# First loads of the outlook on GpSimd, rows measured beside the experts, and two queues in written order

## The chip, the cores and the metric

The kernel runs on one core of a Trainium2 chip. Its time is the device time of that core, in microseconds (us); a comparison takes the median of several runs. TensorE (PE) multiplies and transposes, VectorE (DVE) and ScalarE (ACT) work on whole tiles, GpSimd (POOL) and SyncE (SP) here mostly issue DMAs.

## The reference

Two layers of a vision network on x of 4 x 32 x 32 x 384, in float32. Layer 0 is an attention with a chosen set of keys, then four experts of which each token takes two. Layer 1, where the change lies, is an "outlook" attention and a small feed-forward network whose weights are Kronecker products:

```python
x = x + _L0_conv_ref(_ln_c(x), qkv_w, gp_w, proj_w)      # attention
t = t + _L0_ffn_ref(_ln_t(t), gate_w, gate_b, w1, b1, w2, b2)   # experts: each token takes 2 of 4
x = x + _L1_conv_ref(_ln_c(x), Wv, Wa, Wo)               # outlook
t = t + _L1_ffn_ref(_ln_t(t), c_fc_1, c_fc_2, c_proj_1, c_proj_2)   # Kronecker

# outlook
v = x @ Wv.T ; a = (x @ Wa.T).reshape(b, n, heads, 9, 9)
attn = softmax(a * d ** -0.5)
out[p] = sum over q of attn[p, q] * v[q]   # 3 x 3 patches; q, p are places of a patch
y = sum over p of out[p] shifted by p ; return y @ Wo.T
```

_ln_c is a layer norm over the 384 channels: mean and variance of each row, then (x - mean) / sqrt(variance + eps).

## The kernel before

The 4096 rows of x are 32 tiles of 128 rows, eight tiles to an image. Four stages follow each other: the attention (to about 1290 us), the experts (35 blocks of 256 gathered rows, 31.68 us each, to 2431.6), the outlook (to about 2911) and the Kronecker network (to 3007).

**Experts.** `experts` walks over the blocks. For each it fetches, one block ahead, the weights `up` and `down` with indirect DMAs on GpSimd (`weights`, L1486), the rows (`fetch`, L1507), norms and turns them (`norm` L1516, `turn`), and then multiplies: L1568 with gelu L1572, and L1583, whose result gets its bias at L1588 on VectorE and is stored to `yg` on SyncE (L1589). Weights lie in two sets of buffers, `halves`. Beside the blocks, `add` (L1532) takes a tile of x from `x1`, gathers its two expert rows (`router.gather`, L1452, on GpSimd), adds them with their weights (L1538) and stores the sum to `x2` (L1539). One tile a block is done so, once its image is complete: `done` = 19 tiles. The order of TensorE, VectorE, ScalarE and SyncE in attention and experts is the written one (`manual_schedule`); GpSimd's is set by a planner.

**Between the stages.** `rest` gives places in memory to x of the four images and the weights, then loads them: `fetch(0)`, `wa`, `wv`, `fetch(1)`, `wo`, `fetch(2)`, `fetch(3)`, and the Kronecker weights (`wf` four times, `wp`, `f2` and `p2`), all on SyncE (L95, L2101, L1897 to L1900).

**Outlook.** The planner sets the order on every engine here, from costs and dependencies. The loop at the end of `outlook` walks over 32 steps (image b, tile t), and nine more to drain. In a step:

- `add` (from step 2): one of the 13 tiles that the experts left (tiles 19 to 31) gets its two expert rows, gathered into one of two buffers `yt`, L1665 on VectorE.
- `scores`: norm of the tile (L127), three transposes into `ps_tr` (L135), copy to `xnT` (L136, ScalarE), twelve matmuls to `ps_a` (L1693), of which there is one buffer; maximum and subtraction (L1702, L1703) free it and give `attn`; exponential on ScalarE (L1708), sums, reciprocal and product (L1710 to L1717); `attn` is moved by 32 partitions up and down with three or four DMAs on SyncE (L1729 to L1734); `ps_v` (L1737) and its copy (L1741).
- `band`, two steps later: `u` adds the moved copies (L1750 to L1754), nine small matmuls with the `shift` matrices to `ps_c` (L1758), `co` masks with `inside` (L1766), is written to DRAM (`room`, L1773) and read back skewed (`band`, L1779), both on SyncE.
- `gather`, three steps after that: ps_y (L1795) multiplies band and v; some rows are split, so that narrow matmuls of 66 columns occur.
- `mix`: ps_wo (L1811), and its sum into x (L1815).

The layer norm's statistics are taken for a whole image at a time: `ln_stats` measures eight tiles on VectorE (bn_stats L120, bn_aggr L121), takes the square root on ScalarE (L122) and the reciprocal (L123). For image 0 this is ahead of step 0, for the others in step 4 of the image before:

```python
        stats[0] = net.ln_stats(range(NB), "c")
...
                if t == 4 and b + 1 < B:
                    stats[b + 1] = net.ln_stats(range((b + 1) * NB, (b + 2) * NB), "c")
```

The constants (`shift`, `col`, `inside`) are made on GpSimd and VectorE at the head of `outlook`.

Of the kernel before, what the change touches and what calls it, by code (L numbers as in the profile page):

```python
# [47 lines left out]
class Net:  # L48
# [12 lines left out]

    def slots(self, dram):
# [27 lines left out]
    def load(self, x, tiles=range(NT)):  # L90

        i = tiles.start
        while i < tiles.stop:
            n = min(NB - i % NB, tiles.stop - i)
            self.nc.sync.dma_start(  # L95
# [17 lines left out]
    def stats(self, tiles, key):  # L113

        nc, n = self.nc, len(tiles)
        mv = self.small.tile([P, NT, 2], FP, name="ln_mv", tag="ln_mv")
        rs = self.small.tile([P, NT], FP, name="ln_rs", tag="ln_rs")
# [6 lines left out]
        return mv, rs  # L124

# [1332 lines left out]
def experts(net, router, x1, x2, wup, wdown, beside):  # L1458
# [10 lines left out]
    with ExitStack() as ctx:  # L1469
# [78 lines left out]
        for n in range(NXB):  # L1548
# [27 lines left out]
            if n + 1 < NXB:  # L1576
                norm(n + 1)
            for t in range(TT):
# [17 lines left out]
def outlook(net, wv, wa, wo, left, router, kron):  # L1596
# [15 lines left out]
    with ExitStack() as ctx:  # L1612
# [13 lines left out]
        for dx in (-1, 0, 1):  # L1626
# [34 lines left out]
        def add(i):  # L1661
            for n in range(2):
# [4 lines left out]
                )  # L1667

        stats = {}
# [527 lines left out]
```

## Time and profile before

| what | value |
|---|---|
| runs | 3003.22, 3002.94, 3001.56 us; median 3002.94 |
| profiled execution | 3008.57 us |
| its span | 3006.7 us (1.87 lie around it) |
| mean granted clock of TensorE | 0.971 |
| TensorE busy | 2793.6 us, 93% of the span |
| VectorE, ScalarE, GpSimd busy | 1344.4, 1222.3, 396.4 us |
| outlook | 2431.6 to about 2911 us of the span |

A start time in the profile counts from the begin of the span. A line of the timeline gives start, length, engine, source line, operation, what it writes and reads, sizes and count; in brackets at its end stands how long the engine had been idle before it and what released it. A matmul of 128x486 is a stationary tile of 128 x 128 on 486 columns. `SPq` is SyncE issuing a DMA; a long issue means that the issue itself took that long, not the transfer.

### The profile page before, as it was taken

The page shows a single profiled execution, that of the slowest core. Times are in us where ns is not written, and L with a number is a line of the kernel's source. Part 1 is how long each engine was busy: PE and PEld are TensorE (multiplying, and loading weights), DVE is VectorE, ACT ScalarE, POOL GpSimd, SP SyncE. Part 2 cuts the span into 40 slices and gives each one's busy share as a digit, 9 for nine tenths or more (in the row PEclk, how much of TensorE's full clock was granted, in tenths as well). Part 3 has the DMA queues.
Part 4 walks back from the last instruction along what each step waited for, and adds up shares of the span by engine and source line. Part 5 has one row for each costly group of instructions (what it writes and reads, how often), then busy time and mean ns, then how long its engine had stood idle before and what let it go on. Part 6 is the DMA issues. An engine that isn't in the chain of part 4 may idle for free.

```text
span 3006.7 us, 36661 instructions
## 1 busy us (share of the span) xinstructions
PE 2793.6 (93%) x13236; PEld 1509.9 (50%) x13236; DVE 1344.4 (45%) x3704; ACT 1222.3 (41%) x2026; POOL 396.4 (13%) x496
## 2 busy tenths in 40 slices
PE   6879998999899986689999999999999978999998
PEld 4323333333333331156777777777777744444443
DVE  1466677766776676633010001111111147767652
ACT  3777777776767765321112112111121122222125
POOL 1000000200030004014111112212211012000000
PEclk9989999999999998899999999999999989999999
DMA  5133334322322233254445545555555455544432
GB/s 100 52 81 98 92 92 122 78 54 68 93 56 54 77 90 118 49 200 155 169 177 189 186 174 204 213 211 196 201 215 210 142 170 190 163 165 139 157 112 86
DMA packets 218111, 405.91 MB, mean 135 GB/s; under 512 B 83504, under 2 KB 179296, under 8 KB 204864
## 3 DMA queue, kind: packets, MB, share of 16 engines
q1 hardware_dynamic: 188496, 194.43, 21.7%
q0 software_dynamic: 26432, 206.01, 20.1%
q10 hardware_dynamic: 2992, 3.03, 0.3%
q8 instruction: 107, 1.75, 0.2%
q14 instruction: 84, 0.69, 0.1%
HBM read 305.35 MB, written 49.99 MB: 118 GB/s over the span
## 4 chain that ended last, share of the span: by engine, by line
PE 78%; ACT 7%; DVE 6%; DMA 5%; issue 4%; POOL 0%; SPq 0%; DVEq 0%; POOLq 0%; ACTq 0%
PE ps_h L1568 18%; PE ps_y L1583 17%; PE ps_t L266 7%; PE ps_z L615 7%; PE ps_s L597 6%; PE ps_o L615 5%; PE ps_a L1693 4%; ACT e L607 4%; PE ps_y L1795 3%; DVE e L653 2%; PE ps_wo L1811 2%; DMA yt<-yg,index 2%; PE ps_v L1737 1%; PE ps_h L1964 1%; PE ps_t L400 1%
## 5 line engine op out<-in xcount | busy, mean ns | idle before, releaser
L1572 ACT ACTIVATE h<-ps_h,up 128x256 f32<-128x256 f32 x420 | 199.0, 474 | 929.2 <-PE ps_h L1568 929.2
L1568 PE MATMUL ps_h<-xbT,up 128*128 128x256 f32 x2520 | 556.8, 382 | 0.8 <-DVE xbT L1527 0.7
L1583 PE MATMUL ps_y<-down,h 128*128 128x384 f32 x1680 | 556.8, 489 | 0.0
L1568 PEld LDWEIGHTS ps_h<-xbT,up 128*128 128x128 f32 x2520 | 482.4, 192 | 76.9 <-DVE xbT L1527 1.1
L653 DVE CUSTOM_DVE_ANT_0 e<-e,rz,inv 128x1024 f32<-128x1024 f32 x384 | 474.3, 1272 | 65.1 <-DMA rz<-r_row 64.8
L607 ACT ACTIVATE e<-ps_s,shift 128x1024 f32<-128x1024 f32 x384 | 406.7, 1110 | 192.2 <-PE ps_s L597 191.9
L1583 PEld LDWEIGHTS ps_y<-down,h 128*128 128x128 f32 x1680 | 318.5, 191 | 208.2 <-issue 3.3
L1588 DVE TENSOR_TENSOR y<-ps_y,down 128x384 f32<-128x384 f32 x70 | 39.0, 558 | 755.6 <-PE ps_y L1583 755.6
L615 PE MATMUL ps_z<-e,rt_ones 128*32 128x512 f32 x1536 | 295.1, 631 | 62.8 <-ACT e L607 62.8
L615 PE MATMUL ps_o<-e,wv 128*32 128x512 f32 x1536 | 273.9, 634 | 27.2 <-DVE wv L660 15.6
L597 PE MATMUL ps_s<-q,k 32*128 32x512 f32 x1536 | 222.9, 650 | 0.0
L680 POOL DMA_DIRECT2D q<-po x96 | 75.7, 874 | 1058.2 <-DMA q<-po 622.2
L351 ACT ACTIVATE below<-tk_left,tk_bound 128x1024 bf16<-128x1024 f32 (+1 forms) x160 | 183.8, 1149 | 12.1 <-DVE tk_bound L357 7.6
L1693 PE MATMUL ps_a<-wa,xnT 128*128 128x486 f32 x384 | 172.2, 595 | 10.7 <-DVE attn L1703 10.0
L615 PEld LDWEIGHTS ps_z<-e,rt_ones 128*32 128x32 f32 x1536 | 45.6, 109 | 228.4 <-ACT e L607 190.0
L597 PEld LDWEIGHTS ps_s<-q,k 32*128 32x128 f32 x1536 | 61.5, 187 | 169.5 <-issue 135.1
L615 PEld LDWEIGHTS ps_o<-e,wv 128*32 128x32 f32 x1536 | 66.4, 114 | 150.5 <-issue 108.7
L266 PE MATMUL ps_t<-xnT,wqkv 128*128 128x512 f32 x288 | 138.1, 621 | 2.8 <-ACT tk_left L310 1.8
L1693 PEld LDWEIGHTS ps_a<-wa,xnT 128*128 128x128 f32 x384 | 72.4, 195 | 96.7 <-issue 89.6
L1795 PE MATMUL ps_y<-band,v 128*32 128x194 f32 (+2 forms) x960 | 108.4, 516 | 4.1 <-DMA band<-room 3.9
L1538 DVE SCALAR_TENSOR_TENSOR x<-yt,weight,x 128x384 f32<-128x384 f32 x38 | 23.5, 619 | 191.9 <-DMA x<-x 191.3
L1507 POOL DMA_INDIRECT xb<-x,ids x70 | 66.9, 955 | 251.4 <-PE ps_t L1526 218.4
(331 smaller groups left out, 2860.6 us busy)
## 6 DMA issues: line engine op xcount, KB each, us to landing
band<-room SPq DMA_DIRECT2D x32, 1560.0 KB
rz<-r_row SPq DMA_DIRECT2D x48, 512.0 KB
yg<-y SPq DMA_DIRECT2D x70, 192.0 KB
q<-q SPq DMA_DIRECT2D x192, 64.0 KB
k<-k SPq DMA_DIRECT2D x192, 64.0 KB
room<-none SPq DMA_DIRECT2D x64, 192.0 KB
x<-x SPq DMA_DIRECT2D x38, 192.0 KB
o<-in_x_dram SPq DMA_DIRECT2D x33, 192.0 KB
```

Source lines behind the costliest of these rows:

```text
L266: nc.tensor.matmul(ps, lhsT=lhsT(k), rhs=rhs(k), start=k == 0, stop=k == KC - 1)
L351: nc.scalar.activation(junk[:n], left[:n], AF.Sign, bias=bound[:n], accum_out=over[:n])
L597: nc.tensor.matmul(ps[:, half * 512 : half * 512 + 512], lhsT=self.k4[r, u * P : (u + 1) * P], rhs=self.q4[r, :], start=True, stop=True,)
L607: nc.scalar.activation(e, ps, AF.Exp, bias=shift, scale=QK_SCALE)
L615: nc.tensor.matmul(ps[r : r + 32, :], lhsT=lhsT(odd), rhs=self.es[2 * u + odd][:, half * 512 : half * 512 + 512], start=u == 0, stop=u == ...
L653: nc.vector.tensor_tensor_reduce(self.es[m], self.es[m], self.rz, 1.0, self.im["inv"][:, m, self.h : self.h + 1], ALU.mult, ALU.add, self. ...
L680: nc.gpsimd.dma_start(out=there, in_=po[r : r + 32, :], accum_op=ALU.add)
L1568: nc.tensor.matmul(ps, lhsT=up[:, o : o + P], rhs=xbT[:, k, :], start=k == 0, stop=k == KC - 1,)
L1572: nc.scalar.activation(h, ps, AF.Gelu, bias=up[:, KC * HID + f : KC * HID + f + 1])
L1583: nc.tensor.matmul(ps, lhsT=hs[f][:, t * P : (t + 1) * P], rhs=down[:, f * C : (f + 1) * C], start=f == 0, stop=f == NF - 1,)
L1693: nc.tensor.matmul(pa[:, hh, :HW_], lhsT=xnT[:, k, :], rhs=wa[:, k, hh * HW_ : (hh + 1) * HW_], start=k == 0, stop=k == KC - 1,)
L1795: nc.tensor.matmul(ys[c][32 * n : 32 * n + 32, lo - 512 * half : hi - 512 * half], lhsT=vs[b, t][:, h * HD : (h + 1) * HD], rhs=bands[b, t ...
```

## The change

Four things are done.

1. x of image 0, `wa` and `wv` are loaded on GpSimd's queue. The places in memory are given in another order: Kronecker's small tiles, x of image 0, `wa`, `wv`, `wo`, then the other images.
2. The statistics are taken tile by tile, right after the tile's expert rows are added: for the 19 tiles of the experts in their `add` (`measure`), with one square root and reciprocal in the last block (`scale`); for the other 13 after their `add` in the outlook, with a `scale` whenever an image's tiles are complete. They are kept in `mv` and `rs` for all 32 tiles.
3. In the outlook, SyncE and GpSimd keep the written order (`manual_schedule`); TensorE, VectorE and ScalarE remain with the planner. The remaining loads are written into steps: image 1 and `wo` in step 1, image 2 in step 2, image 3 in step 5, Kronecker's in step 8. So in the written order of SyncE come, in a step, the moves of `attn`, then the step's loads, then `room` and directly `band` of the tile two steps before.
4. The adds of the outlook begin in step 4 instead of step 2, and `col` and `inside` are made after step 0's scores.

Kronecker's own work pool (`kf_work`) is opened in its constructor, and the small buffers of `stats` shrink to its group of 16.

```diff
+        self.mv = cpool.tile([P, NT, 2], FP, name="mv_x2")
+        self.rs = cpool.tile([P, NT], FP, name="rs_x2")
+
...
     def home(self, pool, b):
         self.xs[b] = pool.tile([P, NB, C], FP, name=f"x_{b}", tag=f"x_{b}")
-    def load(self, x, tiles=range(NT)):
+    def load(self, x, tiles=range(NT), queue=None):
         i = tiles.start
         while i < tiles.stop:
             n = min(NB - i % NB, tiles.stop - i)
-            self.nc.sync.dma_start(
+            (queue or self.nc.sync).dma_start(
                 out=self.xs[i // NB][:, i % NB : i % NB + n, :],
                 in_=x[i * P : (i + n) * P, :].rearrange("(t p) c -> p t c", p=P),
             )
...
+
+    def measure(self, pool, i, x):
+
+        st = pool.tile([P, 6], FP, name="x2_st", tag="x2_st")
+        self.nc.vector.bn_stats(st, x)
+        self.nc.vector.bn_aggr(self.mv[:, i, :], st)
+
+    def scale(self, first, last):
+
+        rs = self.rs[:, first:last]
+        self.nc.scalar.activation(rs, self.mv[:, first:last, 1], AF.Sqrt, bias=self.eps["c"])
+        self.nc.vector.reciprocal(rs, rs)
...
                 y = work.tile([P, C], FP, name="yt", tag="yt")
                 router.gather(y, i, n)
                 nc.vector.scalar_tensor_tensor(x, y, router.weight[n][:, i : i + 1], x, ALU.mult, ALU.add)
+            net.measure(work, i, x)
             return lambda: nc.sync.dma_start(out=x2[i * P : (i + 1) * P, :], in_=x)
         added, store = 0, lambda: None
...
                     next(beside, None)
             if n + 1 < NXB:
                 norm(n + 1)
+            else:
+                net.scale(0, added)
             for t in range(TT):
                 if t == TT - 1 and n + 1 < NXB:
                     xbT = turn(n + 1)
...
         inside = const.tile([P, 5 * H6], FP, name="inside")
         col = const.tile([P, 4], FP, name="col")
-        nc.gpsimd.iota(
-            col[:, 0:1], pattern=[[0, 1]], base=0, channel_multiplier=1, allow_small_or_imprecise_dtypes=True,
-        )
-        for r in range(1, P // IMG):
-            nc.vector.tensor_scalar(
-                col[:, r : r + 1], col[:, 0:1], IMG * r - 0.5, -float(IMG), ALU.is_gt, ALU.mult
+        low = const.tile([P, 5 * H6], FP, name="low")
+
+        def columns():
+            nc.gpsimd.iota(
+                col[:, 0:1], pattern=[[0, 1]], base=0, channel_multiplier=1, allow_small_or_imprecise_dtypes=True,
             )
-        for r in range(1, P // IMG):
-            nc.vector.tensor_tensor(col[:, 0:1], col[:, 0:1], col[:, r : r + 1], ALU.add)
-        nc.gpsimd.iota(
-            inside, pattern=[[1, 5], [0, H6]], base=-2, channel_multiplier=0,
-            allow_small_or_imprecise_dtypes=True,
-        )
-        low = const.tile([P, 5 * H6], FP, name="low")
-        nc.vector.tensor_scalar(inside, inside, col[:, 0:1], None, ALU.add)
-        nc.vector.tensor_scalar(low, inside, -0.5, None, ALU.is_gt)
-        nc.vector.tensor_scalar(inside, inside, IMG - 0.5, None, ALU.is_lt)
-        nc.vector.tensor_tensor(inside, inside, low, ALU.mult)
+            for r in range(1, P // IMG):
+                nc.vector.tensor_scalar(
+                    col[:, r : r + 1], col[:, 0:1], IMG * r - 0.5, -float(IMG), ALU.is_gt, ALU.mult
+                )
+            for r in range(1, P // IMG):
+                nc.vector.tensor_tensor(col[:, 0:1], col[:, 0:1], col[:, r : r + 1], ALU.add)
+            nc.gpsimd.iota(
+                inside, pattern=[[1, 5], [0, H6]], base=-2, channel_multiplier=0,
+                allow_small_or_imprecise_dtypes=True,
+            )
+            nc.vector.tensor_scalar(inside, inside, col[:, 0:1], None, ALU.add)
+            nc.vector.tensor_scalar(low, inside, -0.5, None, ALU.is_gt)
+            nc.vector.tensor_scalar(inside, inside, IMG - 0.5, None, ALU.is_lt)
+            nc.vector.tensor_tensor(inside, inside, low, ALU.mult)
         left = list(left)
...
                 nc.vector.scalar_tensor_tensor(
                     net.x(i), y, router.weight[n][:, i : i + 1], net.x(i), ALU.mult, ALU.add
                 )
-
-        stats = {}
+            net.measure(work, i, net.x(i))
+
         attn, vs, bands, ys, moved = {}, {}, {}, {}, {}
         def room(b, t):
...
         def scores(b, t):
             i = b * NB + t
-            mv, rs = stats[b]
             xn = work.tile([P, C], FP, name="xn", tag="xn")
-            net.ln_apply(xn, i, t, mv, rs)
+            net.ln_apply(xn, i, i, net.mv, net.rs)
             xnT = work.tile([P, KC, P], FP, name="xnT", tag="xnT")
             net.transposed(ps_m, "m", xn, xnT, nc.scalar.copy)
             pa = ps_a.tile([P, 2, 512], FP, name="ps_a", tag="a")
...
                 done = b * NB + (4 if half == 0 else 7) + 2 + LAG
                 for n in range(4):
                     at(done + 1 + n // 2, mixed, b, half, n)
-        stats[0] = net.ln_stats(range(NB), "c")
-        t_kron = 0
+        assert left[0] >= 2 * NB
+        t_kron, first = 0, left[0]
         for step in range(B * NB + 9):
             b, t = divmod(step, NB)
-            if step >= 2:
-                for i in left[:1]:
-                    add(i)
-                left = left[1:]
             if b < B:
                 scores(b, t)
-                if t == 4 and b + 1 < B:
-                    stats[b + 1] = net.ln_stats(range((b + 1) * NB, (b + 2) * NB), "c")
+            if step == 0:
+                columns()
+            if step in loads:
+                loads[step]()
+            if step >= 4 and left:
+                add(left.pop(0))
+
+                if left and left[0] % NB == 0 or not left:
+                    net.scale(first, left[0] if left else NT)
+                    first = left[0] if left else NT
             for f, args in later.pop(step, []):
                 f(*args)
             if step == B * NB - 7:
...
         with ExitStack() as late:
-
             pool = late.enter_context(tc.tile_pool(name="late", bufs=1, reuse_waits="tile"))
-            weight = {}
-
-            def home(name, shape):
-                weight[name] = pool.tile(shape, FP, name=name, tag=name)
-
+            kron = Kron(net, late, pool)
             net.xs = {}
-            net.home(pool, B - 1)
-            kron = Kron(net, pool)
             net.home(pool, 0)
-            home("wv", [P, KC, C])
-            kron.home()
-            net.home(pool, 1)
-            net.home(pool, 2)
-            home("wa", [P, KC, 972])
-            home("wo", [P, KC, C])
+            wa, wv, wo = (
+                pool.tile([P, KC, w.shape[-1]], FP, name=n, tag=n)
+                for n, w in (("wa", WaT), ("wv", WvT), ("wo", WoT))
+            )
+            for b in range(1, B):
+                net.home(pool, b)
             def fetch(b):
                 first, last = b * NB, (b + 1) * NB
                 net.load(x2, range(first, min(last, done)))
                 net.load(x1, range(max(first, done), last))
-            def weigh(name, w):
-                nc = tc.nc
-                nc.sync.dma_start(out=weight[name], in_=w.rearrange("(k p) o -> p k o", p=P))
-
-            fetch(0)
-            weigh("wa", WaT)
-            weigh("wv", WvT)
-            for b in range(1, B):
-                fetch(b)
-                if b == 1:
-                    weigh("wo", WoT)
-            kron.load(late, fc1T, fc2, proj1T, proj2)
-            outlook(net, weight["wv"], weight["wa"], weight["wo"], range(done, NT), router, kron)
+            def weigh(queue, tile_, w):
+                queue.dma_start(out=tile_, in_=w.rearrange("(k p) o -> p k o", p=P))
+
+            net.load(x2, range(NB), tc.nc.gpsimd)
+            weigh(tc.nc.gpsimd, wa, WaT)
+            weigh(tc.nc.gpsimd, wv, WvT)
+            loads = {
+                1: lambda: (fetch(1), weigh(tc.nc.sync, wo, WoT)),
+                2: lambda: fetch(2),
+                5: lambda: fetch(3),
+                8: lambda: kron.load(fc1T, fc2, proj1T, proj2),
+            }
+            eng = mybir.EngineType
+            with tc.manual_schedule(engines={eng.SP, eng.Pool}):
+                outlook(net, wv, wa, wo, range(done, NT), router, kron, loads)
             kron.run(out)
     with ExitStack() as outer:
```

More of the change, by code (lines that the diff above doesn't have):

```diff
@@ L115, in stats @@
         nc, n = self.nc, len(tiles)
-        mv = self.small.tile([P, NT, 2], FP, name="ln_mv", tag="ln_mv")
-        rs = self.small.tile([P, NT], FP, name="ln_rs", tag="ln_rs")
+        mv = self.small.tile([P, Kron.GT, 2], FP, name="ln_mv", tag="ln_mv")
+        rs = self.small.tile([P, Kron.GT], FP, name="ln_rs", tag="ln_rs")
         for t, i in enumerate(tiles):
@@ L1593, in experts, with outlook @@
         return added
-def outlook(net, wv, wa, wo, left, router, kron):
+def outlook(net, wv, wa, wo, left, router, kron, loads):
     tc, nc = net.tc, net.nc
@@ L1880, with __init__, load @@
     GT = 4 * QT
-    def __init__(self, net, const):
+    def __init__(self, net, ctx, const):
         self.net, self.tc, self.nc, self.const = net, net.tc, net.nc, const
+        self.work = ctx.enter_context(self.tc.tile_pool(name="kf_work", bufs=2, reuse_waits="tile"))
         self.wf = const.tile([P, HID], FP, name="wf")
-        self.f2 = const.tile([P, self.K], FP, name="f2")
-    def home(self):
-        self.wp = self.const.tile([P, NF, self.A], FP, name="wp")
-        self.p2 = self.const.tile([P, self.K], FP, name="p2")
-    def load(self, ctx, fc1T, fc2, proj1T, proj2):
+        self.f2, self.p2 = (const.tile([P, self.K], FP, name=n) for n in ("f2", "p2"))
+        self.wp = const.tile([P, NF, self.A], FP, name="wp")
+    def load(self, fc1T, fc2, proj1T, proj2):
         nc, A, K = self.nc, self.A, self.K
         const = self.const
-        self.work = ctx.enter_context(self.tc.tile_pool(name="kf_work", bufs=2, reuse_waits="tile"))
         p2 = self.p2
```

## The prediction

> **What bounds the kernel now.** I read the stretches first, then TensorE's timeline where its share drops, then the queue and the engine that its waits name. A line of the stretches gives the stretch, its length, the busy time (and instructions) of PE, PEld, DVE, ACT and POOL, then PE's clock, the DMA share and GB/s.
>
> ```profile
> 2389.00:2401.00 12.00, 12.00 (x44) 7.39 (x43) 1.82 (x4) 0.00 (x0) 0.00 (x0) 1.00 0.04 16
> 2431.60:2446.40 14.80, 0.04 (x1) 0.00 (x1) 7.57 (x31) 0.30 (x1) 0.00 (x0) 0.64 0.90 313
> 2446.40:2560.00 113.60, 98.89 (x402) 49.10 (x403) 85.71 (x215) 30.68 (x56) 24.78 (x26) 0.93 0.64 195
> 2560.00:2670.00 110.00, 110.00 (x465) 52.95 (x466) 77.30 (x191) 24.30 (x47) 0.72 (x2) 1.00 0.50 165
> ```
>
> The experts end at 2431.6 with PE full. PE then stands for 14.8 us while the DMA engines run at 90%; it waits and runs below full clock up to 2560; from there it is full at clock 1.00. So all that the first steps of the outlook lose is time that the end gets, and nothing between 2560 and 2876 can give more. The profiled span is 3006.7.
>
> ```profile
> 2416.00 15.64 PE L1583 MATMUL ps_y<-down,h 128*128 128x384 f32 x48
> 2446.43 0.88 PE L135 MATMUL ps_tr<-ident,xn 128*128 128x128 f32 x3 [14.78 <-DVE xn L127]
> 2447.95 7.57 PE L1693 MATMUL ps_a<-wa,xnT 128*128 128x486 f32 x12 [0.65 <-ACT xnT L136]
> 2459.20 5.05 PE L1693 MATMUL ps_a<-wa,xnT 128*128 128x486 f32 x12
> 2473.10 6.85 PE L1693 MATMUL ps_a<-wa,xnT 128*128 128x486 f32 x12 [2.54 <-DVE attn L1703]
> ...
> 2511.64 1.96 PE L1693 MATMUL ps_a<-wa,xnT 128*128 128x486 f32 x2 [2.98 <-DVE attn L1703]
> ```
>
> The same twelve matmuls take 5.05 us at full clock, 7.57 after the idle 14.78 and 6.85 after an idle 2.54; two of them 1.96 after an idle 2.98, but 1.05 after one of 1.83 (at 2497.10). What PE waits for is VectorE, and VectorE waits for a load:
>
> ```profile
> 2440.80 1.02 DVE L120 BATCH_NORM_STATS2 ln_st<-x 128x6 f32<-128x384 f32 x2 [6.39 <-DMA x<-x]
> ...
> 2445.80 0.87 DVE L127 TENSOR_SCALAR xn<-x,ln_mv,ln_rs 128x384 f32<-128x384 f32 x2
> ```
>
> ```profile
> 2433.42 0.37 SPq L95 DMA_DIRECT2D x<-x  x1
> ...
> 2435.86 6.76 SPq L2101 DMA_DIRECT2D wo<-in_WoT_dram  x1
> ...
> 2454.70 5.79 SPq L1899 DMA_DIRECT2D f<-in_fc_dram  x1
> ```
>
> The load of x comes on SyncE's queue only after the last block's stores; all eight rows of image 0 are measured (2440.80 to 2445.2) before the first is normed. GpSimd had been free for long:
>
> ```profile
> 2369.82 0.94 POOL L1486 DMA_INDIRECT down<-in_wdown_dram,rows_w_all  x1 [15.22 <-DVE y L1588]
> 2401.28 0.36 POOL L1677 MEMSET down<- 32x324 f32 x1 [30.52 <-DVE y L1588]
> ```
>
> The waits of 2431 to 2560 (in total, times, longest):
>
> ```profile
> POOL yt L1452 <- DVE x L1665: 74.6, 18, 30.3
> DVE x L1665 <- DMA yt<-yg,index: 16.0, 9, 4.1
> PE ps_a L1693 <- DVE attn L1703: 10.0, 5, 3.0
> ```
>
> VectorE stands 16.0 us in front of adds whose rows GpSimd has just begun to fetch, and the `attn` (L1703) that frees `ps_a` is queued behind them.
>
> **Start of the outlook.** x of image 0 (1.5 MB), `wa` (1.46 MB) and `wv` (0.58 MB) go to GpSimd's queue right behind the last `down` load, and their tiles no longer lie where the experts' buffers lie, so they can start at about 2371. That load's 2.56 MB ran at 313 GB/s; 3.65 MB more at this rate end near 2371 + 8 + 12 = 2391 to 2395. The stretch 2389:2401 has 4% of DMA in use, and GpSimd's next work was a memset at 2401. Cover: 38 us, from 2395 to 2433. If it were gone, each us late would be a us of idle PE, with the slow clock on top. The Trainium skill speaks against this move: "DMA: Bandwidth & Descriptors", § SWDGE vs HWDGE vs iDMA, gives plain transfers to SyncE or ScalarE, and § Issuing engines are not separate DMA queues says that another engine saves only the issuing time. By that rule alone moving the queue is worth about the 0.4 to 0.6 us of an issue. But the trace shows that the queue decides *when* these loads begin: 60 us earlier. I count by the trace.
>
> With x there and its rows measured, VectorE goes from the last y (2431.68 + 0.56 = 2432.24) over one reduction (0.37) to the first norm: transposes at 2433.3 for 2446.43, ps_a of step 0 at 2434.4 for 2447.95. **13.5 us.** The shift and column work (eight small operations, 1.7 us) moves behind step 0's norm and scores and is needed only at the first `co`, far later.
>
> **Steps 0 to 8, before.** From ps_a(0) to ps_a(9), 2447.95 to 2559.89, are 111.9 us. Work at full clock: nine steps of 0.32 + 5.05 + 1.94 + 1.11 (transposes, ps_a, ps_v, ps_c) = 75.8; four gathers 2.15 + 2.85 + 2.85 + 2.15 = 10.0; 66 narrow ps_y matmuls, 4.0. The other 22.1 are waits (attn 10.0, xnT 3.2, band 0.8) and slow clock: 7.57 - 5.05 = 2.5, 6.85 - 5.09 = 1.8, and some 3.2 after 2511.64.
>
> **The same steps, after.** VectorE has 6.9 us a step for scores (max 2 x 0.58, subtract 2 x 0.58, norm 0.38, rows, sums and reciprocal 1.9, product 1.22, u 0.65, co 0.46), and from step 4 an add 0.53 with its measure 0.53 + 0.17: 8.1 against 8.4 of PE, and 10.6 to 11.3 with a gather. The adds now come one a step from step 4, behind a fetch that was issued two steps earlier (two yt buffers), where before they came in a pack; so the 16.0 of stalls go. Measuring 19 rows moves beside the experts (19 x 0.70 = 13.3 us over 19 blocks of 31.68; VectorE's rows there show 0.5 to 2.0 us in 10 to 12). Cost there: between 0 and, if each stood in PE's way, 13; I take 0, since PE is full in these stretches and the next block's rows are normed well ahead. Walking the written order through these durations gives ps_a(1) 2443.1, (2) 2451.8, (3) 2461.8, (4) 2470.4, (5) 2480.9, (6) 2491.5, (7) 2502.6, (8) 2514, (9) 2525.5: 91.1 us, which is 75.8 + 10.0 of work and 5.3 of waits. The narrow matmuls (4.0) are no longer among it: gathers 0 to 9 stand one step later in PE's new order, so that work is only put off. Gain: 22.1 - 5.3 = **16.8 us.**
>
> Whether a slow clock follows is weighed twice. The skill's "TensorE: Matmul & The Clock Gate", § What's actually happening, puts the drop after a whole idle window of about 3.4 us. By it none of my waits would cost clock, and before only the first would have: the slow part of 16.8 would be 0 to save. The trace has it after 2.54 and 2.98, not after 1.83. By the trace 5.0 of the 22.1 came from waits near 2.5 to 3 us, and go if waits fall below about 2. I take the trace; by the rule the sum were 5 less.
>
> **What it costs.** (1) SyncE keeps the written order: step 1's loads (0.64 + 6.76) stand ahead of up/down(2), the last loads (wf 5.42, wp 0.43, f 5.79, p 1.46: 13.1) in step 8 ahead of room(6), band(6), up/down(9). The long issues came while the DMA engines were full, so less is likely; up/down(9) has roughly a step until `u` needs it: 0 to 5 us, I take 1.4 with anything of this kind. (2) Each band is issued right behind its room write, so SyncE stands 2.65 us there. In the middle this is free: band(12) went at 2648.13, and its gather, behind ps_a(17), ran at 2673.70. (3) At the end it isn't: room(29) was issued at 2875.62, band(29) at 2880.51, both now behind up/down(31) at 2878.59 to 2880.4; band(31), which ended the chain (2890.94), comes behind room(31) behind band(30), about 1 us later. 0 to 3, I take 1. (4) Memsets, square roots (two in the outlook for three), f2's tiny operations: ACT is busy 30.68 of 113.6; 0, at most 1 either way, in the allowance. (5) GpSimd's written order, memsets behind fetches: 0 to 3, I add 1.
>
> Sum: 13.5 + 16.8 - 1.4 - 1 - 1 = **27 us**. Span 3006.7 to about 2980. The profiled run took 3008.57, 5.6 over the median of the runs; the same 27 off 3002.94 give **2976**.
>
> **The rivals.**
> *Only the gap goes.* 13.5, and 2.5 for ps_a(0) at full clock, less the tail's 1: 15, 2988. For it: PE waited for attn five times, and VectorE is busy 75% of that stretch; with PE starting 13 us earlier each step's chain (scores, max, subtract, exponential, product, up/down) has the same length. Against: of VectorE's stretch 16.0 were stalls on fetches, and 24 measures move. 15%.
> *All goes.* Waits near 0 in steps 0 to 8: 13.5 + 22 - 1, some 35 to 37: 2966. Against: the 0.62 to 0.68 waits for xnT are in each early step. 12%.
> *The loads don't start early,* or are hidden anyway. If a tile still waited for an expert buffer, x would come at 2440 as now: within 0.2%. Against: wa, wv and x of image 0 have places of their own. 2%.
> *Slower: the written order of SyncE sets the pace.* The room write (2.65 us) comes to lie on the path of each step, since nothing may pass it: up/down(t+1) behind band(t-2) behind room(t-2) behind co(t-2). 24 steps x 2.65 = 64, less 32 of gain: 3035. It decides once the queue's work per step (up/down 2.55 + room 0.53 + write 2.65 + band 0.33 = 6.1) plus its wait for co passes the 11 to 14 us of a step, or the margin of a band falls below 2.65; net loss from 1.4 us a step on. For it: the first gather waited 0.84 for its band. Against: 6.1 is half a step; band(12) had 25 us. 5%.
>
> **How the numbers follow.** Likeliest case 66%: 2976, its own range 2969 to 2984. All goes 12%, only the gap 15%, same 2%, slower 5%. A measurement of this kernel tells about 0.2% (6 us) from no change. Faster 0.93, same 0.02, slower 0.05. The range 2966 to 2988 leaves out the slower and same cases (7%) and parts of the two outer ones (some 11%).
>
> **What would show it.** Right: x's load on GpSimd at about 2371, landed before 2400; PE's gap after L1583's last matmul under 2 us, ps_a(0) in 5.1 to 5.5 us; the 16.0 wait on yt nearly gone; PE full from about 2525; TensorE's waits of the first nine steps near 5; the last band about 1 us later against ps_a(31). Wrong: waits for attn still near 10 with slow clock behind them (the gap alone), up/down or band among PE's waiters in the middle (the slower case), waits in the last ten expert blocks (measures or loads in the way).

## The result, and the profile after

The changed kernel takes 2992.98 us (median of 15 runs), the kernel before 3007.13 in as many: a ratio of 0.9955, 95% interval 0.9944 to 0.9967. By the ratio, that is 13.5 us less (10 to 17), half of the 27 that were forecast.

The two profiled executions can't be subtracted as they stand. In the one of before the last expert matmul ends at 2431.64 us, in the one of the changed kernel at 2440.44, and the difference is already there where the experts begin (1283.96 and 1292.16), in an attention whose instructions are the same. What the change touches is read from the *last stretch*, from the end of the last expert matmul (L1583 before, L1601 now) to the end of the span: 3006.7 - 2431.64 = 575.1 us before, 2997.0 - 2440.44 = 556.6 now. All times below that begin with "+" count from that end.

The stretches of the changed kernel (columns as before; the experts now end inside the second):

```profile
2389.00:2401.00 12.00, 12.00 (x46) 8.26 (x45) 2.74 (x6) 1.89 (x4) 0.00 (x0) 1.00 0.71 271
2431.60:2446.40 14.80, 12.62 (x39) 6.85 (x38) 4.20 (x16) 0.48 (x1) 0.00 (x0) 1.00 0.11 40
2446.40:2560.00 113.60, 102.43 (x435) 52.03 (x434) 82.07 (x196) 28.07 (x55) 15.07 (x16) 0.97 0.65 199
2560.00:2670.00 110.00, 105.31 (x505) 51.84 (x504) 86.60 (x216) 24.09 (x48) 10.28 (x12) 0.98 0.57 184
```

The loads fill the quiet stretch (271 GB/s where there were 16), and the seam between the stages is closed: PE is busy 12.62 of 14.80 us where it was busy 0.04, at clock 1.00. But the two stretches behind it are not full: 11 us are missing in the first and 4.7 in the second, which was full before. GpSimd's timeline shows when the loads went:

```profile
2378.61 0.94 POOL L1501 DMA_INDIRECT down<-in_wdown_dram,rows_w_all  x1 [15.22 <-DVE y L1606]
2379.55 0.98 POOL L98 DMA_DIRECT2D x<-x  x1
2380.50 0.85 POOL L2113 DMA_DIRECT2D wa<-in_WaT_dram  x1
2381.27 0.84 POOL L2113 DMA_DIRECT2D wv<-in_WvT_dram  x1
...
2429.08 0.99 POOL L1467 DMA_INDIRECT yt<-yg,index  x1 [0.30 <-issue]
2483.70 0.95 POOL L1467 DMA_INDIRECT yt<-yg,index  x1 [53.63 <-DVE x L1685]
```

And TensorE's, the lines that answer to those shown of before:

```profile
2424.80 15.64 PE L1601 MATMUL ps_y<-down,h 128*128 128x384 f32 x48
2441.97 0.52 PE L150 MATMUL ps_tr<-ident,xn 128*128 128x128 f32 x3 [1.53 <-DVE xn L142]
2443.14 5.16 PE L1712 MATMUL ps_a<-wa,xnT 128*128 128x486 f32 x12 [0.64 <-ACT xnT L151]
...
2451.98 5.05 PE L1712 MATMUL ps_a<-wa,xnT 128*128 128x486 f32 x12
...
2493.85 6.17 PE L1712 MATMUL ps_a<-wa,xnT 128*128 128x486 f32 x8 [4.69 <-DVE attn L1722]
```

The idle 14.78 is now 1.53, and ps_a of step 0 takes 5.16 us instead of 7.57. The first five steps run as the forecast walked them, within 0.6 us (+2.7, +11.5, +20.2, +29.8, +38.2). Then step 5 stands: TensorE waits 4.69 us, and the eight matmuls behind it take 6.17 us; eight such take 3.42 at full clock (at 2499.38 in `again`, the second profile of this kernel). VectorE shows why:

```profile
2482.81 0.62 DVE L1685 SCALAR_TENSOR_TENSOR x<-yt,weight,x 128x384 f32<-128x384 f32 x1 [0.17 <-DMA x<-x]
...
2492.51 0.62 DVE L1685 SCALAR_TENSOR_TENSOR x<-yt,weight,x 128x384 f32<-128x384 f32 x1 [5.07 <-DMA yt<-yg,index]
2493.04 0.66 DVE L1722 TENSOR_TENSOR attn<-ps_a,a_max 128x486 f32<-128x486 f32 x1
```

The two rows of tile 19 have held both `yt` buffers since 2429. Its add comes in step 4, at 2482.81, and waits only 0.17 us for its x. Only when it has read the first row does GpSimd fetch for tile 20 (2483.70, after 53.63 of waiting). That fetch takes 8.8 us: a band's read of 1560 KB went out on SyncE 0.2 us before it (2483.47), and in the trace the fetch's first packet moves 4.9 us after its issue, when most of the band has passed. The loads of x are through by then (2482.8). The planner has put the add of tile 20 ahead of the second half of `attn`, which frees `ps_a`, so TensorE waits too. In `again` the same add stands 6.14 us, there on its second row, and TensorE 5.90 us in front of `ps_c`. The waits of the outlook (in total, times, longest), VectorE's for yt and two of TensorE's:

```profile
DVE x L1685 <- DMA yt<-yg,index: 14.9, 6, 5.1
...
PE ps_y L1814 <- DMA band<-room: 6.6, 2, 4.2
...
PE ps_a L1712 <- DVE attn L1722: 6.3, 3, 4.7
```

So 14.9 us are left of the 16.0 that were to go. The band's 6.6 us (3.9 before) lie at the end. SyncE's timeline of the last tiles, and the two DMAs of the chain that it ends in:

```profile
2868.22 1.74 SPq L1792 DMA_DIRECT2D room<-co  x1
2871.89 0.33 SPq L1798 DMA_DIRECT2D band<-room  x1
2873.88 0.37 SPq L1792 DMA_DIRECT2D room<-co  x1
2879.09 0.32 SPq L1798 DMA_DIRECT2D band<-room  x1
2879.50 0.39 SPq L1792 DMA_DIRECT2D room<-co  x1
2886.29 0.32 SPq L1798 DMA_DIRECT2D band<-room  x1
```

```profile
2879.50 6.73 DMA room<-co
...
2886.29 6.26 DMA band<-room
```

Each of the last two room writes is now issued about 2 and 0.4 us behind the read of the band before it: room(30) takes 5.2 us (2873.88 to 2879.09), room(31) 6.73, where the chain of before had 2.65. The packets tell whether the write is slow beside the read or comes late. A room write is 640 packets of 240 B, a band's read 128 of 12,480 B, and both are on SyncE's queue. The DMA view of the time of room(31), 2879.5 to 2884.2 and then 2884.2 to 2886.3:

```profile
DMA packets 120, 1.50 MB, mean 319 GB/s; under 512 B 0, under 2 KB 0, under 8 KB 0
DMA packets 681, 0.26 MB, mean 125 GB/s; under 512 B 672, under 2 KB 672, under 8 KB 672
```

Until 2884.2 not one packet of the write moves; once the read's are nearly through, all of them pass in 1.2 us (2884.44 to 2885.61). So the write stands in the queue behind the read; it is not slowed beside it. In the middle of the outlook a step lies between them: room(28) took 2.6 us (2853.86 to 2856.45).

The last band is issued 33.6 us after ps_a(31) began, before 26.0. Before, it was read together with the one ahead of it and took 10.13 us; now it takes 6.26. So it lands 39.9 us after ps_a(31) began, before 36.2: of the 7.6 us, 3.7 are left.

### The profile page after: what moved, and what is told of

It is laid out like the page before. It is cut to its first block, busy times and chain, and to the rows that moved or that the text cites. A ratio compares the mean times of both kernels' runs of the same rounds, so it can differ in the third digit from the quotient of the medians.

```text
span 2997.0 us, 36619 instructions
## 1 busy us (share of the span) xinstructions
PE 2793.7 (93%) x13236; PEld 1509.3 (50%) x13236; DVE 1349.4 (45%) x3703; ACT 1217.0 (41%) x2023; POOL 399.3 (13%) x499
## 4 chain that ended last, share of the span: by engine, by line
PE 50%; DMA 3%; issue 3%; DVE 3%; ACT 1%; POOL 0%; DVEq 0%; POOLq 0%; ACTq 0%; SPq 0%
PE ps_h L1584 18%; PE ps_y L1601 17%; PE ps_a L1712 4%; PE ps_y L1814 3%; DMA yt<-yg,index 2%; PE ps_wo L1830 1%; PE ps_v L1756 1%; PE ps_h L1984 1%; PE ps_c L1777 1%; PE ps_y L1995 1%; PE ps_t L1541 1%; PE ps_z L630 1%; DMA o<-in_x_dram 1%; PE ps_o L2008 0%; PE ps_o L630 0%
## 5 line engine op out<-in xcount | busy, mean ns | idle before, releaser
L1601 PE MATMUL ps_y<-down,h 128*128 128x384 f32 x1680 | 556.9, 489 | 0.0
L1601 PEld LDWEIGHTS ps_y<-down,h 128*128 128x128 f32 x1680 | 318.5, 191 | 208.2 <-issue 3.5
L1467 POOL DMA_INDIRECT yt<-yg,index x64 | 65.8, 1028 | 289.2 <-DVE x L1553 142.4
```

Source lines behind the costliest of these rows:

```text
L1601: nc.tensor.matmul(ps, lhsT=hs[f][:, t * P : (t + 1) * P], rhs=down[:, f * C : (f + 1) * C], start=f == 0, stop=f == NF - 1,)
```

## The experiments

Each was timed against the kernel before on the same chip. "ps_a(n)" is the begin of the n-th step's scores after the end of the experts, "rest" the time from ps_a(31) to the end of the span. The two profiles of the kernel before agree in the last stretch within 0.4 us, while the begin of the experts shifts between all these profiles by 31 us (1280.2 to 1311.1).

| kernel | ps_a(0) | ps_a(9) | ps_a(31) | rest | last stretch | ratio to before (95%) |
|---|---|---|---|---|---|---|
| before | 16.3 | 128.2 | 433.2 | 141.9 | 575.1 | |
| before_again | 15.7 | 128.5 | 433.5 | 142.0 | 575.5 | 1.0002 (0.9993 to 1.0010) |
| changed | 2.7 | 102.8 | 412.2 | 144.4 | 556.6 | 0.9955 (0.9944 to 0.9967) |
| again (the changed one) | 2.7 | 104.2 | 413.7 | 145.7 | 559.4 | 0.9956 (0.9939 to 0.9973) |
| first_loads_on_sync | 12.5 | 118.2 | 426.8 | 145.7 | 572.5 | 0.9999 (0.9986 to 1.0012) |
| loads_alone | 13.5 | 124.2 | 429.4 | 141.8 | 571.2 | 0.9989 (0.9980 to 0.9998) |
| measure_alone | 12.5 | 123.4 | 425.5 | 142.3 | 567.8 | 0.9971 (0.9958 to 0.9985) |
| measure_at_head | 8.3 | 114.2 | 423.4 | 145.1 | 568.5 | 0.9977 (0.9966 to 0.9987) |
| sync_planned | 2.7 | 107.7 | 419.2 | 142.1 | 561.3 | 0.9959 (0.9943 to 0.9975) |
| tail_pairs | 2.7 | 103.9 | 414.4 | 142.5 | 556.9 | 0.9946 (0.9926 to 0.9966) |
| fetch_ahead | 2.7 | 94.6 | 406.6 | 145.0 | 551.6 | 0.9928 (0.9912 to 0.9943) |
| fetch_and_tail | 2.7 | 94.8 | 407.8 | 142.8 | 550.6 | 0.9925 (0.9910 to 0.9940) |
| fetch_two_ahead | 2.7 | 103.6 | 409.2 | 139.2 | 548.4 | 0.9915 (0.9898 to 0.9932) |

**The two kernels once more.** No edit.

> The changed kernel once more, for the part that lies ahead of the outlook. In the two profiles the last expert matmul ends at 2431.6 us (before) and 2440.4 us (changed), and from there to the end of the span there are 575.1 and 556.6 us. Chance (attention and experts are unchanged in their instructions and only vary from execution to execution): this profile ends its experts anywhere between 2425 and 2445, and its last stretch is again within 2 us of 556.6; time 13 to 18 us under the kernel before. The change slows the attention (other places in memory): experts end at 2440 again, and in every further variant that keeps the change.

> The kernel before once more, for its profile on the chip on which the variants of this call run, and so for what lies ahead of the outlook. In the runs so far the variants that keep the change are 2 to 5 us less fast in time than their last stretch (from the last expert matmul to the end) says against the one profile of before (575.1). Chance: last stretch 572 to 576, and what is missing is scatter of the stages ahead. The change costs something ahead of the outlook: last stretch 575 again, and experts of this run end 3 us or more ahead of those of the variants of this call. Time: ratio 1.000.

The experts of `again` end at 2450.7, outside the window given, on a chip where the kernel before takes 3031.9 us too; on the chip of `before_again` (3005) they end at 2425.9, and those of two variants that keep the change at 2423.7 and 2429.8. So the shift ahead of the outlook belongs to chip and execution. The last stretch of the changed kernel scatters more than expected (556.6, 559.4), that of before less (575.1, 575.5). In time the change is worth 13.5 us (10 to 17) in the first comparison and 13.3 (8.2 to 18.5) in this one, by the last stretches 15.7 to 18.9. The lower of these lies within both intervals, the upper one outside both; the gap of 2 to 5 us was not settled.

**The stall on the fetch.** Edit, with `start` the first of the 13 tiles:

```diff
-                y = bp.tile([P, C], FP, name="yt", tag="yt", bufs=2)
+                k = 2 * (i - start) + n
+                y = kron.wf[:, k * C : (k + 1) * C] if k < 4 else bp.tile([P, C], FP, name="yt", tag="yt", bufs=2)
```

> The first two adds of the outlook (tiles 19 and 20) fetch into the still empty tile of wf instead of the two buffers yt, so that the fetch of tile 20 does not wait for the add of tile 19, and that of tile 21 does not wait for 20. Theory stall (VectorE stands in front of an add whose fetch began only when the add before it ended; 5.07 us there, then 4.69 us of TensorE and 2.8 of slow clock in step 5): the waits of VectorE for yt fall from 14.9 to under 6, the 4.69 goes, last stretch 556.6 - 5 to 9 = 548 to 552, time 5 to 9 us under the changed kernel. Theory written order of SyncE (room writes and loads hold the queue): the wait of step 5 comes back at another place, last stretch within 2 us of 556.6.

Last stretch 551.6, ratio 0.9928, some 8 us in time better than the changed kernel on the same chip: the stall in step 5 was the fetch's wait for its buffers. SyncE's written order is as in the changed kernel, and the wait did not come back at another place: behind the first transposes TensorE has none above 1 us up to ps_a(9). GpSimd issues all four fetches at the head (the third and fourth, for tile 20, are shown), and in step 5 tile 20's add on VectorE no longer waits:

```profile
2448.10 0.95 POOL L1467 DMA_INDIRECT wf<-yg,index  x1 [0.30 <-issue]
2449.35 0.95 POOL L1467 DMA_INDIRECT wf<-yg,index  x1 [0.30 <-issue]
```

```profile
2505.18 0.58 DVE L1687 SCALAR_TENSOR_TENSOR x<-wf,weight,x 128x384 f32<-128x384 f32 x1
2505.68 0.65 DVE L1724 TENSOR_TENSOR attn<-ps_a,a_max 128x486 f32<-128x486 f32 x1
```

ps_a(9) is at +94.6. The forecast's walk, which had no stall in it, said 2525.5 - 2431.6 = +93.9, where the changed kernel has +102.8. VectorE still waits 8.6 us for later fetches (2.6 at most), since these again begin one add ahead.

**The tail.** Edit: in the last step, band(30) is issued behind room(31).

```diff
+            if b * NB + t != B * NB - 2:
+                for back in ((1, 0) if b * NB + t == B * NB - 1 else (0,)):
+                    m = bands[b, t - back] = bp.tile([P, BAND, NH], FP, name="band", tag="band")
+                    nc.sync.dma_start(
...
```

> In the last step SyncE issues room(30), room(31), band(30), band(31) instead of room(30), band(30), room(31), band(31). Theory tail (the last room write shares the DMA engines with the read of the band before it and takes 6.8 us instead of 2.65): the last band is issued 4 to 6 us earlier against ps_a(31); last stretch 2 to 4 us shorter, 553 to 554.5; time 2 to 4 us under the changed kernel. Rival (the two bands read together take longer, 10.1 us as in the kernel before, and gather(29) is bound by up/down(31) anyway): last stretch within 1 us of 556.6.

```profile
2892.49 2.58 SPq L1792 DMA_DIRECT2D room<-co  x2
2898.42 0.81 SPq L1800 DMA_DIRECT2D band<-room  x2
```

Both rooms go out together, and the last band about 27 us after ps_a(31) (2871.9) instead of 33.6; it lands 37.5 us after it, for 40.6 in `again`. The rest is 142.5 for the 145.7 of `again` on this chip: 3.2 us back. The expectation's cause, a write that shares the engines, was not right: the packets show a write that waits behind the read, and the edit takes one such wait out. The table says it more broadly: all five profiles with SyncE's written order to the end have a rest of 144.4 to 145.7, the five with the planner's order 141.8 to 142.3, `tail_pairs` and `fetch_and_tail` 142.5 and 142.8 (the third with the edit, `fetch_two_ahead`, is below). In time (0.9946 for 0.9956) the step is too small to be told.

**Both edits.**

> Both edits at once: tiles 19 and 20 fetch into wf's empty tile, and the last two rooms are written ahead of the last two bands. The two costs lie at different places (steps 4 to 9, and behind the last scores), so they should add: last stretch 551.6 - 2.5 = 548 to 550, ratio 0.992. If they were one and the same wait that moves about, the last stretch stays at 551 to 553.

550.6, a little over the window; the front of one (94.8) and the rest of the other (142.8) stand side by side, so these are two separate costs. Of the two, only the first shows clearly in the time.

**The first loads back on SyncE.** Edit: `tc.nc.gpsimd` becomes `tc.nc.sync` in the three loads.

> x of image 0, wa and wv are loaded on SyncE again, behind the experts' last stores; all else as changed. The gap step of the prediction: TensorE's idle ahead of the first transposes comes back from 1.5 to about 10 us (14.8 of the kernel before less the 4.4 us in which eight rows were measured, since these are measured beside the experts), with a slow clock in ps_a(0) (2.5); last stretch 556.6 + 10 to 12 = 567 to 569. Rival (the lead is given back later, for steps 3 to 9 are held by loads, fetches and bands and not by where step 0 began): last stretch 556.6 to 562.

```profile
2470.22 0.87 PE L150 MATMUL ps_tr<-ident,xn 128*128 128x128 f32 x3 [9.34 <-DVE xn L142]
2473.43 6.99 PE L1712 MATMUL ps_a<-wa,xnT 128*128 128x486 f32 x12 [2.34 <-DMA wa<-in_WaT_dram]
```

All of the gain in time is gone. x is issued 1.8 us after the end of the experts (2462.66), where the changed kernel issues it 60.9 us ahead of it (2379.55). The idle 9.34 is as expected; wa comes late as well (2.34), and the matmuls behind it are slow (6.99). Last stretch 572.5, 13 to 16 us over the changed kernel and some 4 over the window. The rival that a lead is given back later fell: 9.8 us are lost at ps_a(0), and 13 to 15 at ps_a(31).

**The loads alone, in the kernel before.** The places in memory are moved as in the change; of the edit, the loads:

```diff
-            fetch(0)
-            weigh("wa", WaT)
-            weigh("wv", WvT)
+            net.load(x2, range(NB), tc.nc.gpsimd)
+            weigh("wa", WaT, tc.nc.gpsimd)
+            weigh("wv", WvT, tc.nc.gpsimd)
```

> The kernel before with one part of the change: x of image 0, wa and wv loaded on GpSimd, in the changed kernel's places in memory; eight rows measured at the head of the outlook as before, planner's order on all engines. Gap: 14.8 becomes 5 to 7 (eight measures 4.4 and the root), with a slow clock still behind it in ps_a(0) (an idle above 2.5). Theory that the parts add (loads 8 to 9, rows measured beside the experts another 4.4 + 2.5 of slow clock): last stretch 575.1 - 8 to 10 = 565 to 567, ratio 0.997. Rival (given back in the first steps, which are held by the adds and by the statistics of image 1): last stretch above 570.

The last stretch gains only 3.9 us, ratio 0.9989: x was there, but the gap stayed at 11.9. On VectorE the planner put a row of image 1, still loaded by SyncE, in front of the last aggregation of image 0, and everything behind it waited:

```profile
2438.91 0.56 DVE L120 BATCH_NORM_STATS2 ln_st<-x 128x6 f32<-128x384 f32 x1 [3.37 <-DMA x<-x]
```

My window (565 to 567) was wrong since it took the eight measures for all that stood there.

**The measuring alone, in the kernel before.** Edit: `measure` and `scale` as in the change, loads and order as before.

> The kernel before with the measuring alone: the 19 rows are measured beside the experts, the other 13 after their adds; loads on SyncE, planner's order, adds from step 2 as before. Theory (the gap has two members in series, the load of x on SyncE behind the last stores and the eight measures behind it; taking out the second leaves the first): the gap is 14.8 - 5.0 = 9 to 10 us, still with the slow clock behind it; and the 24 measures of images 1 to 3 that lay in a pack in front of the scores are gone or spread; last stretch 575.3 - 5 to 8 = 567 to 570, ratio 0.998. Cost beside the experts: 0. Rival (measuring beside the experts costs time there, 19 x 0.7 us standing in TensorE's way, and was what kept the change's time 2 to 5 us behind its last stretch): last stretch as above but ratio 1.000 or more, with expert blocks longer than 1149 us in all.

```profile
2465.93 0.87 PE L149 MATMUL ps_tr<-ident,xn 128*128 128x128 f32 x3 [9.26 <-DVE xn L141]
2469.13 6.97 PE L1709 MATMUL ps_a<-wa,xnT 128*128 128x486 f32 x12 [2.33 <-DMA wa<-in_WaT_dram]
```

Gap 9.26, last stretch 567.8, some 9 us less by the ratio (0.9971). The expert blocks last 1146.5 us in all, 1145.7 and 1147.7 in the two profiles of the kernel before: the measures cost nothing there that shows. `first_loads_on_sync` has items 2 to 4 of the change, so the measuring and the written order and later adds too, and gains nothing (572.5, 0.9999). So without the early loads, what comes on top of the measuring costs some 5 us, 3.4 of them in the rest.

**The loads on GpSimd, the measuring at the head.** Edit in the changed kernel: tiles 0 to 7 are not measured beside the experts.

```diff
+        for i in range(NB):
+            net.measure(work, i, net.x(i))
+        net.scale(0, NB)
```

> The changed kernel, but the eight rows of image 0 are measured at the head of the outlook (behind the loads on GpSimd) and not beside the experts; nothing of image 1 is measured there. Theory (the gap goes only when both of its members go, the load and the measuring; the loads alone left 11.9 us of it since the planner put image 1's rows, which came late, among those of image 0): the gap is 1.5 + 8 x 0.53 + root and reciprocal 0.7 + 0.3 = 6.5 to 7.5 us, ps_a of step 0 runs at the slow clock (7.5 instead of 5.1), so last stretch 7 to 9 us longer than the changed kernel's 556.6 to 559.4: 564 to 567, ratio 0.998. Rival (the first steps have slack behind the gap, so part is caught up by step 9): 560 to 562.

```profile
2454.32 0.87 PE L150 MATMUL ps_tr<-ident,xn 128*128 128x128 f32 x3 [6.79 <-DVE xn L142]
2455.84 7.58 PE L1713 MATMUL ps_a<-wa,xnT 128*128 128x486 f32 x12 [0.65 <-ACT xnT L151]
```

The gap is 6.79, and the matmuls behind it are slow: 7.58. The last stretch is 568.5, 9 to 12 us over the changed kernel, again somewhat more than expected. So the gap has its members in series: the load, then the measures, and a slow ps_a(0) behind what is left of them. Only with load and measures both gone is the gap 1.53, and ps_a(0) then ran at full clock in all of these profiles but one (`fetch_two_ahead`, below).

**SyncE left to the planner.** Edit: `engines={eng.Pool}`.

> SyncE's order in the outlook is left to the planner again, GpSimd keeps the written one; all else as changed. All later loads (x of images 1 to 3, wo, wf) then go at the head of the outlook, and the tail has its two rooms ahead of its two bands. Theory written order costs little in the middle and 2.5 us in the tail: steps 0 to 9 within 2 us of the changed kernel except that tile 19's x is there earlier, which alone does not help since the fetch of tile 20 still waits for its add; last stretch 553 to 558. Rival (the written order is what keeps SyncE free for the moves of attn in the first steps, where the loads stood ahead of them in the kernel before): steps 0 to 3 lose 5 to 15 us to loads ahead of up/down, last stretch 560 to 570.

Up to ps_a(31) the written order is a gain, but not for the reason that I gave. The planner loads image 2 early and then puts the add of tile 19 into the first step, where its x has not landed:

```profile
2438.40 1.27 DVE L1685 SCALAR_TENSOR_TENSOR x<-yt,weight,x 128x384 f32<-128x384 f32 x2 [10.37 <-DMA x<-x]
```

```profile
2442.95 7.25 PE L1712 MATMUL ps_a<-wa,xnT 128*128 128x486 f32 x11 [6.91 <-DVE mv_x L133]
```

Step 1 begins at +19.3 for +11.5. Its rest is 142.1, so the written order is worth 5.5 to 7 us up to ps_a(31) (419.2 for 412.2 and 413.7) and costs 2.3 to 3.6 at the end. In time (0.9959) it can't be told from the changed kernel.

**A version meant to beat both.** Every fetch two steps ahead of its add, in six places; Kronecker's loads in step 18; the tail's edit.

```diff
+                k = (2 * (i - start) + n) % 6
+                y = kron.wf[:, k * C : (k + 1) * C] if k < 4 else bp.tile([P, C], FP, name="yt", tag="yt", bufs=2)
...
+            if step >= 2 and start + step - 2 < NT:
+                fetch(start + step - 2)
...
-                8: lambda: kron.load(fc1T, fc2, proj1T, proj2),
+                18: lambda: kron.load(fc1T, fc2, proj1T, proj2),
```

> A version meant to beat both: every add's fetch is issued two steps ahead of the add (three pairs of places: four in wf's tile, two yt), the Kronecker loads go to step 18 so that wf's tile stays free until then, and the last two rooms are written ahead of the last two bands. Theory stall: VectorE's waits for yt, 14.9 in the changed kernel and some 10 to 12 with only the first two fetches ahead, fall under 2; the waits of TensorE in steps 10 to 12 for the sums behind ps_wo (4.5 us with two tiles ahead), which stand on VectorE behind such adds, fall under 2; last stretch 545 to 549, against 550.6 with the first two fetches and the tail; ratio 0.990 to 0.992. Rival (the waits of steps 10 to 12 come from the three uses of two small PSUM buffers, not from the adds): last stretch 549 to 551.

548.4, ratio 0.9915 (0.9898 to 0.9932), about twice the gain of the change. No add waits for its fetch any more, and TensorE waits for nothing that shows between +103 and +245. But that it beats `fetch_and_tail` (0.9925) is not shown. Its ps_a(31) comes at 409.2, later than 407.8 there. Its lead lies in the rest (139.2), and not in the tail's order: the last band lands 37.3 us after ps_a(31), as in `tail_pairs` (37.5). In Kronecker's stage, 60 to 80 us after ps_a(31), its granted clock was 1.00, where the profiles with SyncE's written order or the tail's edit had 0.81 to 0.89; I estimate 2 to 3 us from these shares of the clock, and none of the edits touches that stage.

In front it is 9 us behind `fetch_ahead` at ps_a(9) (103.6 for 94.6). Some 6 of these lie at two places: ps_a(0) was slow behind an idle of 1.53, and a wait for `u` of 3.00 us came up in step 5, with slow matmuls after it (granted clock 0.57 in the first 3.2 us of ps_a(0), 0.53 from 2511.4 to 2515.0):

```profile
2455.18 0.52 PE L150 MATMUL ps_tr<-ident,xn 128*128 128x128 f32 x3 [1.53 <-DVE xn L142]
2456.34 6.85 PE L1720 MATMUL ps_a<-wa,xnT 128*128 128x486 f32 x12 [0.65 <-ACT xnT L151]
...
2510.41 0.54 PE L1785 MATMUL ps_c<-u,shift 128*128 128x180 f32 x2 [3.00 <-DVE u L1781]
...
2511.46 3.43 PE L1720 MATMUL ps_a<-wa,xnT 128*128 128x486 f32 x4
```

At full clock the twelve take 5.16 (2443.14 in the changed kernel, behind the same 1.53) and the four 1.79 (2511.91 in `fetch_ahead`). What delays that `u` was not tried.

## Why the prediction was half right

*The gap, 13.5.* Right: ps_a(0) moved from +16.3 to +2.7, 13.6. That it takes load and measuring together was implied, not said; alone they give 3.9 and 7.3 of last stretch. Cover and landing of the loads were right: they were issued right behind the last down load, at 2379.6 where about 2371 was forecast, in an execution whose experts end 8.8 us later.

*The queue.* The Trainium skill's "DMA: Bandwidth & Descriptors" (§ SWDGE vs HWDGE vs iDMA) would have plain loads on SyncE or ScalarE, and taken for a rule would have kept the loads where they cost 13 us here (0.9999 for 0.9956). The trace's reading, that the queue decides when they begin, held: 60.9 us ahead of the experts' end on GpSimd, 1.8 behind it on SyncE.

*Steps 0 to 8, 16.8.* This is the term that failed. ps_a(9) came 25.4 us earlier, not 34.4; less the put-off 4.0 and the gap's 13.6 that is 7.8 for 16.8. The wrong step is that the adds would come "behind a fetch that was issued two steps earlier (two yt buffers)" and that "so the 16.0 of stalls go". Two buffers hold the two rows of *one* tile: the next tile's fetch begins when the add before it has read its row. I counted buffers and not what a tile takes of them. 14.9 us of the 16.0 stayed. With four more places for the first two tiles the walk was met within 1 us (94.6 for 93.9), so the rest of the walk was right.

*The slow clock.* The prediction took its trace (slow after waits of 2.54 and 2.98 us, not after 1.83) against the window of about 3.4 us in "TensorE: Matmul & The Clock Gate" (§ What's actually happening). The later runs bear out neither as a limit on a single wait. Waits below 1.83 were followed by slow matmuls: 1.53 in `fetch_two_ahead`, and 1.43 in `tail_pairs`, while 1.53 in the same step of `again` was not. And in `before_again` 3.21 cost nothing. The lines of `tail_pairs`, `again` and `before_again`:

```profile
2548.28 6.85 PE L1712 MATMUL ps_a<-wa,xnT 128*128 128x486 f32 x12 [1.43 <-DVE attn L1722]
...
2543.51 5.16 PE L1712 MATMUL ps_a<-wa,xnT 128*128 128x486 f32 x12 [1.53 <-DVE attn L1722]
...
2520.34 1.05 PE L1693 MATMUL ps_a<-wa,xnT 128*128 128x486 f32 x2 [3.21 <-DVE attn L1703]
```

The granted clock agrees: 0.52 in the first 3.2 us behind the 1.43, and 1.00 behind the 1.53 and the 3.21. So the length of the last wait does not decide it, and what does is not shown here. For the sum it mattered little: behind the 4.69 of the stall, longer than either number, the slow matmuls cost 2.75 more (6.17 - 3.42).

*The end, 1.* Measured 2.5 to 3.8: I priced the wait behind the room write with the 2.65 us of the old chain, in which the band ahead of it had been read by then. In the new order the last two room writes stand in the queue behind a band's read.

*The rest.* SyncE's loads 1.4, GpSimd's order 1: nothing of this kind is seen apart from the stall. The last loads took 1.99 + 0.39 + 1.28 + 0.43 = 4.1 us of issuing, for 13.1 before: less, as guessed. The measures beside the experts cost 0, as forecast.

With the measured terms, 13.6 + 7.8 - 2.5 = 18.9, against 575.1 - 556.6 = 18.5 of last stretch; 7.8 is itself a difference, so this only says that nothing large lies elsewhere. Why the time shows 13.5 and not 18.5 stays open. That 13.5 is also the gap's term, and near the 15 of the rival "only the gap goes", is chance. That rival's reason, a VectorE whose chain of work sets the pace, does not hold: with the fetches ahead (`fetch_ahead`) the steps follow the walk, and in the changed kernel steps 0 to 4 show no wait of TensorE for `attn` above 1 us.

## What to carry to other kernels

When a change gives an engine an earlier start, walk the first thing that each queue waits for, with the buffers counted in the units in which they are used: two buffers for a pair of rows are one slot. Side work on an engine that keeps its order (here the adds on VectorE) should find its data fetched; otherwise it stops what stands behind it. And where writes and reads share one queue, look at what is ahead of each write: with a band's read just ahead, the same write landed 6.73 us after its issue instead of 2.65.

## What was not expected of the hardware

The same write of 150 KB into `room` landed 2.65 us after its issue in the tail of before and 5.2 to 6.7 behind a band's read of 1.56 MB on the same queue, though its own packets passed in 0.9 to 1.7 us each time. A fetch of 192 KB on the other queue, GpSimd's, was late too when a band's read had gone out just before it: 8.7 us from issue to landing, where the quickest of the changed kernel's twenty took 3.0. And equal idles of TensorE (1.53 us) were followed by full clock in one execution and by a slow one in another.

The kernel before takes 3005 us on one chip and 3031 to 3032 on two others (0.9%); the changed kernel's two profiles begin their experts at 1292.2 and 1304.1, but differ by only 2.8 us in the last stretch. Most of such a difference lies ahead of the part that was changed, and has to be taken out before two profiles are compared.
